# Every transfer on one queue: dt and dt·u stored chunk by chunk, and a schedule drawn anew

## The chip, the core and the metric

The kernel runs on one core of one Trainium2 chip. The core has a matrix engine (PE, with its weight loads PEld), a vector engine (DVE), an activation engine (ACT), a general engine (POOL) and a queue engine (SP) that only issues transfers. They work side by side, each in the order in which its instructions were written, and wait for each other through semaphores. Transfers are issued by SP, ACT or POOL and carried out by 16 DMA engines. The metric is the device time of one execution in microseconds.

## The reference, cut to what matters

The input is x, 4 x 384 x 32 x 32. Two layers follow each other, each with a state-space scan and a feed-forward part, with layer norms and residual sums around them.

```python
# layer 0: four scan directions over 1024 positions, 384 channels, 16 states
x_dbl = einsum('bkdl,kcd->bkcl', xs, x_proj_weight)         # dt rows, B, C
dt = softplus(einsum('bkrl,kdr->bkdl', dts, dt_projs_weight) + bias)
def step(h, inp):
    dtt, ut, bt, ct = inp
    dA = exp(dtt[..., None] * A)
    h = h * dA + (dtt * ut)[..., None] * bt[:, :, None, :]
    return h, einsum('bkdn,bkn->bkd', h, ct)
# ... sum of directions, layer norm, gelu; then t + ffn(ln(t))
# layer 1: in_proj to 2 x 768, causal conv of 4 taps, silu, the same scan over
# 768 channels, * silu(z), out_proj, layer norm; then a mixture of experts:
# softmax gate over 4 experts, the best 2, gelu(x w1 + b1) w2 + b2, weighted sum
```

Everything is in float32.

## The kernel before, in words

**The scan.** The work of both layers' scans is cut into 48 passes. A pass is one batch item, one direction (layer 0) or one group of 384 channels (layer 1), and one half of 512 positions. A pass has three chunks of 128 channels, and a chunk has four steps, each for 4 of the 16 states; that makes 576 steps. In a step the 128 partitions hold 32 channels x 4 states, and four quarters x of the chunk's channels lie side by side. The step consists of

- POOL: `s = dtus * bt` (L1778, called b),
- ACT: `da = exp(dts * a)` for each of the four quarters (L1784, a decay), into one PSUM bank per quarter,
- DVE: one scan per quarter (L1793), then the products with `ct` (L1842); POOL takes one or two of the four products instead (L1858), as the planner decides,
- PE: four sums over the states into `acc` (L1814). After the chunk's last step DVE gathers `acc` (L666 to L672, L918).

**The data of a pass.** `prep_quad0` and `prep_quad1` make, once for two passes, the rows dt, B and C of a direction by a matmul on PE (L637 with the weights `wx0`; L899 in layer 1). ACT copies the result to `xd` (L642), and `rows_out` (L491) stores it to DRAM. `ask_quad0` (L648) loads `wx0` for the next quad as soon as the pass it depends on is prepared; `wx0` has one buffer. `prep_pass` (L520) makes dt (PE L529, softplus in several ACT passes, and a sum on DVE L562 or PE), and dt·u on POOL (L568), each as a tile of 128 x 3 x 512. `spread_out` (L511) stores such a tile in DRAM in the order in which the steps read it, in four transfers of 192 KB, each of 32 partitions and all three chunks. `spread_pass` (L575) loads them back, spread over the states: dt·u of a chunk in one transfer of 1 MB on SP (L590, two buffers), dt of a chunk in two halves of 512 KB on ACT's queue (L596, three buffers). The second half of a chunk goes into the buffer that the first half of the chunk before has used, so it can be asked for only after the second decay of that chunk's last step.

**The order.** Nothing is ordered by hand. `Plan` (L167) draws up the program: it knows a duration for every step, keeps a time for each engine, and emits, one after the other, the instruction that can start first. The scan's own instructions are streams; all else (norms, convolutions, feed-forward, experts, the preparation of passes) are side steps, written as generators that say `yield engine, duration` before they emit. A side step goes in where the planner sees room. `land(kb)` is the planned time of a transfer. `Free` hands out buffers. `fill` adds small matmuls (L1833) to PE's planned gaps. What the planner decides is only the order on each engine; on the chip, semaphores do the waiting. The transfers of SP and ACT take eight completion semaphores in turn, so a transfer is issued only once the eighth before it has landed.

**The experts.** Their blocks (L1386, L1420, L1442) run beside the scan as far as there is room. What is left after the last scan step runs alone at the end, with weights that SP loads (L1355).

Of the kernel before, what the change touches and what calls it, by code (L numbers as in the profile page):

```python
# [133 lines left out]

class Lane:
# [18 lines left out]
    def ready(self):  # L154
        return max(self.want[2] if len(self.want) > 2 else self.end, self.floor) + SLACK[self.rank >= LOW][self.want[0]]
# [11 lines left out]
class Plan:  # L167
# [4 lines left out]
    def __init__(self, streams, jobs, choose, fill):  # L172
# [4 lines left out]
        self.now = 0.0  # L177
        self.stuck = 0.0
# [28 lines left out]
    def mains(self, e):  # L207

        out = []
        for k in range(len(self.streams.get(e, ()))):  # L210
            op = self.head(e, k)
            if op is not None and all(d in self.end for d in op.deps):
                t = max([self.end[d] + LAG for d in op.deps], default=0.0) + op.lag
                out.append((max(self.free[e], t), k, op))
        return out
# [18 lines left out]
    def run(self):  # L234
        while True:
# [22 lines left out]
            start, what, e = best  # L258
            self.stuck = max(self.stuck, start)
# [4 lines left out]
            if isinstance(what, Lane):  # L264
                cost = what.want[1]
# [4 lines left out]
                what.go(what.end, start)  # L270
            else:
# [4 lines left out]
                op.emit()  # L276


@with_exitstack
def layers(ctx, tc, ins, out, const):  # L280
# [160 lines left out]

    def layernorm(src, dst, eps, sq=None, sq_at=0.0, centred=False, scaled=True):
# [41 lines left out]
    def wload(src):  # L484
# [3 lines left out]
        nc.sync.dma_start(out=w.rearrange("p c m -> p (c m)"), in_=src)  # L488
        return w

    def rows_out(q, to):  # L491

        q["rows"] = q.get("rows") or dram.tile([2 * NS, L], F32, tag="rows", name="rows", bufs=4)
        nc.scalar.dma_start(out=q["rows"][:, to], in_=xd[q["at"] : q["at"] + 2 * NS, to])
# [12 lines left out]
    def load_dtw(q, k):  # L507

        nc.sync.dma_start(out=dtw[dt_rows(q), :], in_=ins["w_dt1"][:, k * D : (k + 1) * D])

    def spread_out(to, of):  # L511

        for q in range(NG):
            nc.sync.dma_start(out=to[:, :, q, :].rearrange("c r t -> r c t"), in_=of[q * QP : (q + 1) * QP])
# [5 lines left out]
    def prep_pass(v, p, of_u):  # L520
# [25 lines left out]
        if sums_on_pe(v):  # L546
            yield ACT, 1.5
            nc.scalar.activation(dtu, dtu, AF.Ln, bias=1.0)
            for c in range(NC):
# [6 lines left out]
                ps.give(pd)  # L556
        for c in () if sums_on_pe(v) else range(NC):
# [6 lines left out]
        spread_out(spread[0], dt)  # L564
        for c in range(NC):
            yield POOL, 1.3 if len(of_u(dt[:, c, :], c)) == 1 else 1.75
            for (to, u), (by, _) in zip(of_u(dtu[:, c, :], c), of_u(dt[:, c, :], c)):
                nc.gpsimd.tensor_tensor(to, by, u[:, c], ALU.mult)  # L568
        tmp.give(dt)
        t = yield SP, land(768)  # L570
        spread_out(spread[1], dtu)
# [3 lines left out]
    def spread_pass(p):  # L575
# [3 lines left out]
        def gen():  # L579
            spread, stored = st.pop(("spread", p))  # L580
            for part in range(NC):
# [8 lines left out]
                nc.sync.dma_start(out=dtus[n % 2].rearrange("p q t -> p (q t)"), in_=of(1, 0, NG))  # L590
                plan.end["dtu", p, part] = plan.now + land(1024)
                for x in range(2):
                    m = 2 * n + x - 3
                    before = (yield from until(("da", 4 * (m // 2) + 3, 2 * (m % 2) + 1))) if m >= 0 else 0.0
                    yield ACT, 0.55, max(before, stored)
                    nc.scalar.dma_start(out=dts[(2 * n + x) % 3].rearrange("p q t -> p (q t)"), in_=of(0, 2 * x, 2))  # L596
# [5 lines left out]
    def prep0(b):  # L602
        u = st[("u0", b)]

        def ln(h):
            def gen():
                yield SP, land(768)
                nc.sync.dma_start(out=u[h], in_=half(x_in[b], h))
# [20 lines left out]
    def prep_quad0(q, b, k):  # L629
        def gen():  # L630
# [9 lines left out]
            for h in range(NT):  # L640
                yield ACT, 0.6
                nc.scalar.copy(xd[q["at"] : q["at"] + QROW + R0, cols(h)], px[h * HP : h * HP + QROW + R0])  # L642
            rows_out(q, slice(0, L))
            ps.give(px)
# [3 lines left out]
    def ask_quad0(q, k):  # L648
        def gen():
            yield SP, land(66)  # L650
            nc.sync.dma_start(out=wx0.rearrange("p c m -> p (c m)"), in_=ins["w_x0"][k])
            nc.sync.dma_start(out=dtw[dt_rows(q), :], in_=ins["w_dt0"][k])
# [21 lines left out]
    def post0(b, h):  # L674
# [15 lines left out]
        def add_x(c):  # L690
            def gen():
                xh = yield from t1.take()
                yield SP, land(256)
                nc.sync.dma_start(out=xh, in_=piece(x_in[b], c, h))
# [8 lines left out]
        def ln2():  # L703
# [8 lines left out]
            nc.sync.dma_start(out=fold[:, :, :32], in_=fold_d)  # L712
# [14 lines left out]
        def ffn(lane):  # L727
            def gen():
# [6 lines left out]
                for i in range(2 * lane, 2 * lane + 2):  # L735
                    w, proj1 = yield from wts.two()
                    yield SP, land(192) + 2.0
                    nc.sync.dma_start(
                        out=w.rearrange("p a m -> p (a m)")[zrow, :], in_=ins["w_fc1"][:, i * NC * P : (i + 1) * NC * P]
                    )  # L740
                    nc.sync.dma_start(
# [29 lines left out]
        def ffn_out():  # L771
# [4 lines left out]
            nc.sync.dma_start(out=spread.rearrange("p a m -> p (a m)"), in_=of)  # L776
# [12 lines left out]
            nc.sync.dma_start(out=half(x1[b], h), in_=y)  # L789
# [11 lines left out]
    def prep1(b, h):  # L801
# [6 lines left out]
        def conv(i):  # L808
            def gen():
                for j in range(NC):  # L810
# [8 lines left out]
                    nc.sync.dma_start(out=dg, in_=taps_d[c])  # L819
# [33 lines left out]
        def gate(i):  # L853
            def gen():
# [14 lines left out]
                nc.scalar.dma_start(out=to.rearrange("(c p) t -> p c t", p=P), in_=z)  # L869
# [16 lines left out]
    def prep_quad1(q, b, h):  # L886
        def gen():
# [3 lines left out]
            nc.sync.dma_start(out=wx1, in_=ins["w_x1"].rearrange("p (c m) -> p c m", c=NI))  # L891
# [1215 lines left out]
```

## Time and profile before

| | us |
|---|---|
| three runs | 5034.54, 5049.6, 5051.74 (median 5049.6) |
| the profiled execution | 5032.81 |
| its span, first to last instruction | 5031.0 |
| busy in the span: PE, DVE, POOL, ACT | 4262.9, 4159.0, 4006.4, 3037.3 |
| scan steps (about 110 to 4515 us): DVE busy | 4072.76 of 4405 |
| last experts (4515 to 5031 us): PE busy | 509.12 of 516 |

The transfers move 899.33 MB, 179 GB/s over the span. SP's queue carries 704.28 MB of them (q1) and ACT's 166.22 MB (q10). The page gives for each group of instructions its busy time, the mean of one, and the idle time of the engine just before them with what ended it; a line such as `A <- B: 92.5, 39, 14.1` in the list of waits says that A waited for B 92.5 us in all, in 39 places, at most 14.1 us at once.

### The profile page before, as it was taken

To read this page: it belongs to the slowest core of one execution; us is meant where nothing else is said; L and a number is where in the kernel's file an instruction comes from. 1 tells how busy PE (TensorE), PEld (TensorE's weight loads), DVE (VectorE), ACT (ScalarE), POOL (GpSimd) and SP (SyncE) were. 2 spreads that over 40 slices of the span, in tenths; PEclk is the share of its full clock that TensorE was granted. 3 is DMA by queue.
4 is the path that set the end of the run, shared out by engine and by line. 5 is a ranking of instruction groups with operands and counts; after the bars stand their busy time and mean duration, and the time that the engine had idled before them with its cause. 6 is when DMAs were issued, how large, how long until landed. Compare 5 with 4: busy or idle time off the path is not lost. (4 is left out here: it accounts for less than half of the span.)

```text
span 5031.0 us, 57132 instructions
## 1 busy us (share of the span) xinstructions
PE 4262.9 (85%) x17967; PEld 2192.9 (44%) x17967; DVE 4159.0 (83%) x5754; ACT 3037.3 (60%) x4769; POOL 4006.4 (80%) x1826
## 2 busy tenths in 40 slices
PE   8777778887767799988877798899888888899999
PEld 3222222222223454444444454345534333569996
DVE  4999999999999899999989999999999999850002
ACT  4544458765545577767654577767685756554442
POOL 2999999999988898989988988889899988850002
PEclk9887889888888899999987899899988889899998
DMA  4344656654443565556564655466655454655556
GB/s 148 110 161 156 205 169 214 207 185 139 161 143 107 195 193 175 190 188 211 188 221 161 215 181 175 155 197 205 230 179 191 155 181 148 220 184 180 170 165 190
DMA packets 394191, 899.33 MB, mean 179 GB/s; under 512 B 62384, under 2 KB 143520, under 8 KB 375456
## 3 DMA queue, kind: packets, MB, share of 16 engines
q1 hardware_dynamic: 336672, 704.28, 43.3%
q10 hardware_dynamic: 49024, 166.22, 9.7%
q0 software_dynamic: 8192, 25.17, 1.6%
q8 instruction: 143, 2.34, 0.2%
q14 instruction: 160, 1.31, 0.1%
HBM read 712.11 MB, written 183.40 MB: 178 GB/s over the span
## 5 line engine op out<-in xcount | busy, mean ns | idle before, releaser
L1778 POOL TENSOR_TENSOR s<-dtus,bt 128x2048 f32<-128x2048 f32 x576 | 2605.3, 4533 | 178.1 <-PE acc L1814 67.2
L1784 ACT ACTIVATE da<-dts,a 128x512 f32<-128x512 f32 x2304 | 1530.2, 686 | 886.4 <-DVE s L1842 771.5
L1814 PE MATMUL acc<-s,four 128*32 128x512 f32 x4608 | 735.1, 682 | 382.0 <-POOL s L1858 344.9
L1858 POOL TENSOR_TENSOR s<-s,ct 128x512 f32<-128x512 f32 (+1 forms) x552 | 942.5, 1708 | 138.6 <-DVE s L1793 102.0
L1793 DVE TENSOR_TENSOR_SCAN da<-da,s 128x512 f32<-128x512 f32 x775 | 918.2, 1216 | 114.0 <-ACT da L1784 82.4
L1842 DVE TENSOR_TENSOR s<-da,ct 128x512 f32<-128x512 f32 x1529 | 1009.6, 680 | 0.1
L1793 DVE TENSOR_TENSOR_SCAN da<-da,state,s 128x512 f32<-128x512 f32 x754 | 939.5, 1277 | 17.7 <-ACT da L1784 10.1
L1833 PE MATMUL acc<-ident,few 128*32 128x256 f32 x2886 | 751.5, 416 | 36.2 <-DVE big L918 18.6
L1833 PEld LDWEIGHTS acc<-ident,few 128*32 128x32 f32 x2886 | 334.4, 119 | 510.6 <-issue 225.1
L1793 DVE TENSOR_TENSOR_SCAN s<-da,state,s 128x512 f32<-128x512 f32 x398 | 495.5, 1267 | 8.7 <-ACT da L1784 8.6
L1793 DVE TENSOR_TENSOR_SCAN s<-da,s 128x512 f32<-128x512 f32 x377 | 447.1, 1204 | 17.3 <-ACT da L1784 17.3
L1814 PEld LDWEIGHTS acc<-s,four 128*32 128x32 f32 x4608 | 106.5, 113 | 748.9 <-POOL s L1858 547.3
L1420 PE MATMUL ps<-tmp,mw 128*128 128x256 f32 (+1 forms) x1812 | 387.9, 369 | 22.3 <-ACT tmp L1465 11.5
L1442 PE MATMUL ps<-mw,tmp 128*128 128x192 f32 x2096 | 377.1, 337 | 17.5 <-DMA mw<-in_w_dram 6.8
L1442 PEld LDWEIGHTS ps<-mw,tmp 128*128 128x128 f32 x2096 | 350.4, 195 | 82.4 <-issue 42.9
L1420 PEld LDWEIGHTS ps<-tmp,mw 128*128 128x128 f32 x1812 | 316.5, 198 | 135.7 <-issue 30.4
L1615 DVE SCALAR_TENSOR_TENSOR big<-big,gk,da 128x384 f32<-128x384 f32 x2 | 1.2, 612 | 414.2 <-PE da L1613 414.2
L1605 POOL DMA_INDIRECT big<-ys,slot x12 | 11.8, 980 | 382.7 <-DMA ys<-t 379.3
L799 PE MATMUL ps<-big,w 128*128 128x512 f32 x576 | 280.2, 627 | 14.3 <-DMA w<-in_w_in_dram 8.2
L568 POOL TENSOR_TENSOR tmp<-tmp,big 128x256 f32<-128x256 f32 (+1 forms) x186 | 193.0, 1063 | 68.3 <-DVE tmp L1037 68.3
L529 PE MATMUL ps<-xd,dtw 12*128 12x512 f32 (+1 forms) x288 | 187.9, 743 | 17.2 <-ACT tmp L542 9.4
L838 PE MATMUL ps<-tmp,t 128*128 128x512 f32 x368 | 175.3, 620 | 15.6 <-ACT tmp L830 9.9
(448 smaller groups left out, 5322.2 us busy)
## 6 DMA issues: line engine op xcount, KB each, us to landing
mw<-in_w_dram SPq DMA_DIRECT2D x414, 384.0 KB
dts<-dts ACTq DMA_DIRECT2D x288, 512.0 KB
dtus<-dts SPq DMA_DIRECT2D x144, 1024.0 KB
dts<-tmp SPq DMA_DIRECT2D x376, 192.0 KB
bt<-rows SPq DMA_DIRECT2D x192, 256.0 KB
ct<-rows SPq DMA_DIRECT2D x192, 256.0 KB
dts<-in_w_dram SPq DMA_DIRECT2D x78, 384.0 KB
ys<-t SPq DMA_DIRECT2D x32, 768.0 KB
```

The source lines that it names most:

```text
L529: nc.tensor.matmul(pd, lhsT=dtw[dt_rows(q), c * P : (c + 1) * P], rhs=xd[dt_rows(q), cols(h)], start=True, stop=True,)
L568: nc.gpsimd.tensor_tensor(to, by, u[:, c], ALU.mult)
L799: nc.tensor.matmul(pi, lhsT=w[:, c, :], rhs=u[:, c], start=c == 0, stop=c == NC - 1)
L1420: nc.tensor.matmul(ph[:, k * width : (k + 1) * width], lhsT=w[:, c, k * P : (k + 1) * P], rhs=turned[:, c], start=c == 0, stop=c == NC - 1,)
L1442: nc.tensor.matmul(py[:, k * HD : (k + 1) * HD], lhsT=by_f(hids[half_], width)[:, at_, k * P : (k + 1) * P], rhs=w[:, f], start=4 * q + f ...
L1778: nc.gpsimd.tensor_tensor(ss[i % NSR], dtus[part_of(i) % 2], rep(bts[i % 4], NG), ALU.mult)
L1784: nc.scalar.activation(das[x], dts[(2 * part_of(i) + x // 2) % 3][:, x % 2, :], AF.Exp, scale=v["a"][:, g, m : m + 1])
L1793: nc.vector.tensor_tensor_scan(d if in_psum else s, d, s, 0.0 if v["first"] else state[:, v["slot"], j, x : x + 1], ALU.mult, ALU.add)
L1814: nc.tensor.matmul(acc[x * QP : (x + 1) * QP, :], lhsT=four, rhs=ss[i % NSR][:, x, :], start=m == 0, stop=m == 3)
L1833: nc.tensor.matmul(acc[:QP, : 2 * P], lhsT=nil.to_broadcast([P, QP]), rhs=rep(ident, 2), start=fresh, stop=fresh)
L1842: nc.vector.tensor_tensor(ss[i % NSR][:, x, :], das[x], cts[i % 4], ALU.mult)
L1858: nc.gpsimd.tensor_tensor(s[:, m:, :], s[:, m:, :], rep(cts[i % 4], NG - m), ALU.mult)
```

## The change

All transfers but the indirect ones of POOL are issued by SP: the dt loads, the stores of `rows` and the stores of `z` leave ACT's queue. Each is issued through `ask`, which also tells a model of the queue, `Ring`, about it: SP needs 0.55 us to issue a transfer in the plan, and a transfer can't be issued before the eighth one before it has landed. The planner takes that into account when it asks when SP is free. `spread_out` stores one chunk of 128 channels at a time (256 KB, 128 partitions, with the four quarters as the outer dimension in DRAM), as soon as that chunk is made. In the preparation of a pass the next chunk's step then follows the planned end of the store before it. The planned time of a transfer is slightly shorter, and every side step's duration in the plan is multiplied by a random factor between 0.99 and 1.01 (seed 9; twelve such draws exist).

```diff
+class Ring:
+    at = busy = 0.0
+    lands = [0.0] * 8
+    n = 0
...
+    def next(cls):
+        return cls.lands[cls.n % 8] + 0.1
...
+    def issue(cls, kb):
+        t = max(cls.at, cls.next())
+        cls.busy = max(t + 1.2, cls.busy) + kb / RATE
+        cls.lands[cls.n % 8] = cls.busy + 1.0
+        cls.n += 1
+        cls.at = t + ISSUE
+SEED, SPREAD = 9, 0.02
...
     def ready(self):
-        return max(self.want[2] if len(self.want) > 2 else self.end, self.floor) + SLACK[self.rank >= LOW][self.want[0]]
+        least = Ring.next() - LAG if self.want[0] == SP or len(self.want) > 3 else 0.0
+        return max(self.want[2] if len(self.want) > 2 else self.end, self.floor, least) + SLACK[self.rank >= LOW][self.want[0]]
...
-                cost = what.want[1]
+                cost = what.want[1] * (1.0 + SPREAD * (self.draw.random() - 0.5))
...
+                self.free[e] = max(self.free[e], Ring.at) if Ring.at > start else self.free[e]
...
+    def ask(queue, out, in_):
+        Ring.issue(int(np.prod(out.shape)) / 256)
+        queue.dma_start(out=out, in_=in_)
...
-        nc.scalar.dma_start(out=q["rows"][:, to], in_=xd[q["at"] : q["at"] + 2 * NS, to])
+        ask(nc.sync, out=q["rows"][:, to], in_=xd[q["at"] : q["at"] + 2 * NS, to])
...
-    def spread_out(to, of):
-        for q in range(NG):
-            nc.sync.dma_start(out=to[:, :, q, :].rearrange("c r t -> r c t"), in_=of[q * QP : (q + 1) * QP])
+    def spread_out(to, of, c):
+        ask(nc.sync, out=to[c].rearrange("r q t -> q r t"), in_=of[:, c])
...
                 nc.scalar.copy(dt[:, c, :], pd)
                 ps.give(pd)
+                yield SP, land(256)
+                spread_out(spread[0], dt, c)
...
             nc.vector.tensor_tensor(dt[:, c, :], dt[:, c, :], pd, ALU.add)
             ps.give(pd)
-        spread_out(spread[0], dt)
+            made = plan.free[DVE]
+            yield SP, land(256), made
+            spread_out(spread[0], dt, c)
...
                 nc.gpsimd.tensor_tensor(to, by, u[:, c], ALU.mult)
+            t = yield SP, land(256)
+            spread_out(spread[1], dtu, c)
         tmp.give(dt)
-        t = yield SP, land(768)
-        spread_out(spread[1], dtu)
...
-                    yield ACT, 0.55, max(before, stored)
-                    nc.scalar.dma_start(out=dts[(2 * n + x) % 3].rearrange("p q t -> p (q t)"), in_=of(0, 2 * x, 2))
+                    yield SP, land(512), max(before, stored)
+                    ask(nc.sync, out=dts[(2 * n + x) % 3].rearrange("p q t -> p (q t)"), in_=of(0, 2 * x, 2))
...
-            rows_out(q, slice(0, L))
             ps.give(px)
+            yield SP, land(128)
+            rows_out(q, slice(0, L))
...
-                nc.scalar.dma_start(out=to.rearrange("(c p) t -> p c t", p=P), in_=z)
+                yield SP, land(768)
+                ask(nc.sync, out=to.rearrange("(c p) t -> p c t", p=P), in_=z)
...
 def land(kb):
-    return 3.5 + kb / 200
+    return 3.2 + kb / 220
+RATE, ISSUE = 220.0, 0.55
```

Every other `nc.sync.dma_start` becomes `ask(nc.sync, ...)` with the same operands.

## The prediction

> **What bounds the kernel now.** First the page's busy shares and slices, then the stretches, then the waits.
>
> ```profile
> span 5031.0 us, 57132 instructions
> PE 4262.9 (85%) x17967; PEld 2192.9 (44%) x17967; DVE 4159.0 (83%) x5754; ACT 3037.3 (60%) x4769; POOL 4006.4 (80%) x1826
> ...
> DVE  4999999999999899999989999999999999850002
> ```
> ```profile
> 110.00:4515.00 4405.00, 3663.59 (x14969) 1716.39 (x14970) 4072.76 (x5444) 2772.59 (x4326) 3942.11 (x1763) 0.89 0.55 180
> 4515.00:5031.00 516.00, 509.12 (x2711) 439.78 (x2709) 42.68 (x125) 214.72 (x361) 43.14 (x43) 0.96 0.58 175
> ```
>
> Columns of the second: stretch, length, busy PE, PEld, DVE, ACT, POOL, granted clock, DMA share, GB/s. There are two stages. For 4405 us the 576 scan steps run: DVE is busy 4073 us and sets the pace (7.65 us a step), POOL 3942 us. Then 516 us of expert blocks, in which PE alone is busy (99%). DVE idles 332 us in the first stage. That is what the change can win, and any new wait of DVE is what it can lose. Who makes DVE wait:
>
> ```profile
> ACT xd L642 <- PE ps L637: 106.8, 14, 15.7
> ...
> PE ps L637 <- DMA wx<-in_w_x_dram: 93.8, 12, 14.9
> DVE da L1793 <- ACT da L1784: 92.5, 39, 14.1
> ...
> ACT da L1784 <- DMA dts<-dts: 35.0, 14, 6.5
> ```
>
> (total us, times, longest). The first three are one chain. Its longest case, from the timeline of four engines:
>
> ```profile
> 1664.21 8.83 SPq L514 DMA_DIRECT2D dts<-tmp  x4
> 1673.09 0.43 SPq L651 DMA_DIRECT2D wx<-in_w_x_dram  x1
> ```
> ```profile
> 1675.43 5.41 PE L637 MATMUL ps<-big,wx 128*44 128x256 f32 x24 [12.04 <-DMA wx<-in_w_x_dram]
> ```
> ```profile
> 1680.88 0.58 ACT L642 COPY xd<-ps 44x512 f32<-44x512 f32 x1 [15.65 <-PE ps L637]
> ```
> ```profile
> 1683.57 2.35 DVE L1793 TENSOR_TENSOR_SCAN da<-da,s 128x512 f32<-128x512 f32 x2 [14.12 <-ACT da L1784]
> ```
>
> POOL finishes the three dt·u products at 1662.2; SP needs 8.8 us for four stores, then asks for wx; PE waits for it, ACT waits in order at the xd copy with the next decays behind it, and DVE runs dry. Ten of the layer-0 quads cost DVE 4.8 to 14.1 us in this way, 77 us together (gaps of DVE beside those copies).
>
> **The change part by part.**
>
> (a) ACT no longer issues 328 transfers. Rows: 288 at 0.52 us (L596), 24 at 0.33 (L494), 16 z stores at about 0.4: 165 us of ACT's queue. ACT is busy 63% of the first stage, so this is mostly cover for nothing; DVE waits on ACT for 118 us (92.5 and 25.8), of which 55 belong to the quads. ACT's work in front of DVE becomes 6% less: -8 us (0 to -20).
>
> (b) The quad chain. In the changed order the products of a pass no longer stand in one run on POOL but one per scan step, each followed by its own store, and wx is asked for after one store of 256 KB instead of four of 192 KB. In the trace, wx lands 8.4 us after the last product in the ten bad cases (5.4 to 13.1); with one store (0.4 us of issue) and wx (0.5) I expect about 7. But the order moves PE's quad and ACT's copy as far as it moves POOL: before, the copy stands 0.2 steps behind POOL's last product in the ten bad cases and 1.0 to 9.5 steps behind it in the four good ones; after, it stands -0.5 to +0.5 steps behind in thirteen of fourteen. So the ten win 1.4 us each, and quads 8, 15 and 18, which had room, lose it (3 x about 6 us). +5 us; ends -77 (all ten go) and +50.
>
> (c) The dts loads, 512 KB, now on SP. The first halves have room: 24.5 us (median) from landing to use. The second halves don't: their buffer is free only after the second decay of the chunk's last step. Today ACT issues them 0.03 us (median) later, they land in 5.45 us (90%: 8.23), and DVE would notice if the landing came 5.8 us later (median; 2.9 for the tightest tenth). From these 144 margins, one lateness for all costs DVE 5.5 us at 2 us, 16 at 3, 43 at 4, 87 at 5, 151 at 6. Two things make them late. *Queueing on SP*: SP serves in order, so a load waits for whatever its predecessors wait for, and behind it wait dtus, ct and mw loads. By position in the order, only 6 of the 144 stand behind a producer that is later than the decay that frees their buffer, each by at most half a step; so this is small. *The stores*: their DRAM side now has an outer dimension of 4. The trace has such a transfer: w<-spread_d (192 KB, eight times) is completed by five semaphore increments where others have sixteen, so four channels carry it, and it lands in 5.70 us (median) where w<-in_w_in_dram, of the same size, takes 3.74. A 2048-byte packet takes 0.105 us, so 288 stores put 32 x 0.105 x 288 = 968 us on four channels, where 384 stores put 6 x 0.105 x 384 = 242 us on each of sixteen. Mean share of those four in the first stage: 0.55 + 726/4405 = 0.71. A dts load now waits about 1.8 us (5.45 less the fastest 3.67); as share/(1 - share) this doubles, 2 us more. If the extra is scattered exponentially with mean 2 us, the margins give 144 tight loads 30 us; with mean 1, 5 us; with mean 4, 153. I take +30, ends 0 and +153.
>
> [...]
>
> (d) The chunk stores lengthen the preparation of a pass, for each next chunk waits in the schedule for the last one's store. POOL's last product comes 0 to 4 steps (before: 3 to 7) ahead of the freeing of the buffer for the pass's first dtus load in most passes. A store of 6 us and a load of 7.1 us are two steps, and POOL runs 2.5 steps ahead of DVE, so that covers. Passes 24, 26 and 46, 4 to 5 steps late today, cost 6.8, 2.0 and 12.6 us; after, 24, 26 and 34 are 3 late, 46 is 4, 47 is 2. 0 us (-20 to +30).
>
> (e) Last stage: after the last scan sum PE has 8 more expert matmuls (0.337 us) and 4 transposes: +3 us. The rest there is the same.
>
> (f) Rows and z stores on SP, `ps` given back earlier, 83 fewer filler matmuls, 4% fewer transfers: off the path, 0. They are covered by PE's idle time (4405 - 3664 us) and SP's waits; were that cover gone, 83 x 0.42 = 35 us of PE.
>
> (g) Durations drawn anew by up to 1%: the instructions' counts per engine stay within 0.1% on DVE (1527 products for 1529), so only small stalls move: 0 +- 20.
>
> **Sum.** -8 + 5 + 30 + 0 + 3 = +30 us on the profiled 5032.8 us (span 5031.0), so 5063. The median of the runs shown, 5049.6, is 17 us above that execution; on it, 5080.
>
> **The rivals.** R1, the four channels become the bound: second halves land 4 to 5 us later throughout (+43 to +87), wx 3 us later in 13 quads (+39), so about +95 net: 5145. For it: DMA shares of 0.6 and more in 13 of the 40 slices, where the four would stand above 0.75; each issue also needs the eighth transfer before it to have landed (SP waited 58.7 us for dts loads at the stores). Against: the six stores of a pass are now a step apart. It decides once the second halves land in over 10 us.
> R2, the other side: the schedule now reckons with SP's issue time and its eight transfers in flight, and the quads' stalls go (-77), with (c) as forecast: -8 - 77 + 30 + 3 = -52: 4998. For it: PE's quads stand mostly two to six scan sums later. Against: POOL's products moved as far. It decides if ACT comes to the copy over 12 us after the last product (today 1 to 11).
> R3, spaced stores disturb nothing: -8 + 5 + 3 = 0: 5050.
> That the change doesn't do what it says is excluded by the order: no transfer is left on ACT, 288 stores stand singly.
>
> **How the numbers follow.** My sum 0.40 (its own range 5050 to 5115), R1 0.20, R2 0.20, R3 0.20. About 25 us (0.5%) is what a measurement tells from no change. Faster by more: R2 0.20, R3 0.04, the sum's low end 0.03: 0.27. Within: R3 0.12, the sum 0.14: 0.26. Slower: the rest, 0.47. The range leaves out 0.08 below R2's middle less 10, and 0.1 above R1: 4985 to 5150.
>
> **What would show it.** Right: ACT has no transfers; ACT's wait for dts grows from 35 us to 60 to 120; wx waits of PE stay at 70 to 130 us; stores end with four increments and land in over 5.5 us; the last stage stays 515 to 522 us. Wrong: DVE's gaps at the xd copies gone (R2), or dts waits of several hundred us (R1).

## The result, and the profile after

The changed kernel takes 5054.9 us (median of 21 runs, 5043.2 to 5067.1) where the kernel before takes 5040.4 (median of 21 runs, 5030.6 to 5053.7). The ratio is 1.0026, with a 95% interval of 1.0017 to 1.0035: about 13 us slower. The forecast was 5080 with a range of 4985 to 5150, 30 us above the kernel before. So the sign was right and the size less than half of the forecast; the working behind it was right in less than that, as the experiments show.

The page of the changed kernel, with busy shares and DVE's slices:

```profile
span 5050.0 us, 56868 instructions
PE 4243.3 (84%) x17801; PEld 2178.2 (43%) x17801; DVE 4163.3 (82%) x5756; ACT 3031.5 (60%) x4769; POOL 4013.6 (79%) x1847
...
DVE  3999999999998899999999889999999999950002
...
q1 hardware_dynamic: 380704, 870.48, 52.5%
```

There is no queue of ACT any more, q1 (SP) carries what the two carried. DVE's busy time is nearly the same (4163.3 us for 4159.0), and so is the shape of the slices. The stretches, with the columns as before (stretch, length, busy PE, PEld, DVE, ACT, POOL, clock, DMA share, GB/s):

```profile
110.00:4515.00 4405.00, 3613.55 (x14670) 1682.05 (x14668) 4082.36 (x5452) 2766.31 (x4323) 3951.88 (x1790) 0.89 0.54 179
```

The same 4405 us hold 10 us more of DVE's work mostly because the scan stage now reaches further. Measured by its own marks it is this, in us of the profiled executions:

| | before | after | |
|---|---|---|---|
| first scan starts | 99.4 | 102.5 | +3.1 |
| first scan to last scan | 4373.3 | 4383.1 | +9.8 |
| last scan to the end | 558.3 | 564.4 | +6.1 |
| DVE's gaps over 0.3 us in the scan stage | 276.4 | 280.4 | +4.0 |
| of these beside the xd copies of layer 0 | 77.5 | 67.3 | -10.2 |

The waits, for the whole span:

```profile
DVE da L1840 <- ACT da L1831: 112.9, 45, 29.4
...
ACT xd L686 <- PE ps L681: 105.4, 16, 12.0
...
PE ps L681 <- DMA wx<-in_w_x_dram: 77.8, 13, 9.1
...
ACT da L1831 <- DMA dts<-dts: 46.8, 16, 8.6
```

The chain wx, quad, xd copy, decay, scan is there as before (93.8, 106.8 and 92.5 us then). The 29.4 us of the first line is one wait ahead of the first scan; before, DVE waited there 23.6 us for POOL. ACT's wait for the dts loads rose from 35.0 to 46.8 us and not to the 60 to 120 us that were forecast. One quad of the changed kernel, from the timeline of four engines:

```profile
455.00 0.52 SPq L481 DMA_DIRECT2D dts<-tmp  x1
455.62 0.42 SPq L481 DMA_DIRECT2D wx<-in_w_x_dram  x1
...
461.49 5.40 PE L681 MATMUL ps<-big,wx 128*44 128x256 f32 x24 [8.09 <-DMA wx<-in_w_x_dram]
...
466.93 1.17 ACT L686 COPY xd<-ps 44x512 f32<-44x512 f32 x2 [8.81 <-PE ps L681]
...
468.73 2.34 DVE L1840 TENSOR_TENSOR_SCAN s<-da,s 128x512 f32<-128x512 f32 x2 [4.89 <-ACT da L1831]
```

SP is quick now: one store, and wx is asked for 0.6 us later. But PE starts only 5.9 us after that. From issue to landing, by the trace's completion events, wx takes 6.06 us in the median (2.80 before), and a store 7.11 (3.85 before, for 192 KB). In all 14 quads that come behind a store, wx lands just after that store, 0.2 us later (0.17 to 0.35). The store ends with five increments, one about 1 us after the issue and four from 5.4 us on. Of wx's sixteen, twelve come before those four in each of the 14, and the last four 0.17 to 0.56 us behind them. DVE loses 4.9 us here.

From the time and the totals of the waits alone one would say: nothing much happened, rival R3 came, spaced stores disturb nothing. That reading is wrong.

### The profile page after: what moved, and what is told of

It reads as the page before. It is cut to its first block, busy times and chain, and to the rows that moved or that the text cites. A ratio compares the mean times of both kernels' runs of the same rounds, so it can differ in the third digit from the quotient of the medians.

```text
span 5050.0 us, 56868 instructions
## 1 busy us (share of the span) xinstructions
PE 4243.3 (84%) x17801; PEld 2178.2 (43%) x17801; DVE 4163.3 (82%) x5756; ACT 3031.5 (60%) x4769; POOL 4013.6 (79%) x1847
## 5 line engine op out<-in xcount | busy, mean ns | idle before, releaser
L1861 PE MATMUL acc<-s,four 128*32 128x512 f32 x4608 | 722.4, 671 | 364.3 <-POOL s L1905 348.8
L1880 PE MATMUL acc<-ident,few 128*32 128x256 f32 x2720 | 713.0, 416 | 62.1 <-DVE big L965 26.8
L1880 PEld LDWEIGHTS acc<-ident,few 128*32 128x32 f32 x2720 | 313.1, 119 | 513.9 <-issue 213.5
L1489 PE MATMUL ps<-mw,tmp 128*128 128x192 f32 x2152 | 397.8, 341 | 8.5 <-ACT tmp L1535 5.9
L1489 PEld LDWEIGHTS ps<-mw,tmp 128*128 128x128 f32 x2152 | 367.2, 199 | 85.6 <-issue 42.2
L612 POOL TENSOR_TENSOR tmp<-tmp,big 128x256 f32<-128x256 f32 (+1 forms) x183 | 191.8, 1061 | 75.8 <-DVE tmp L1084 66.9
L844 PEld LDWEIGHTS ps<-big,w 128*128 128x128 f32 x576 | 111.5, 205 | 190.5 <-issue 139.2
```

The lines of the kernel that those rows point to most:

```text
L844: nc.tensor.matmul(pi, lhsT=w[:, c, :], rhs=u[:, c], start=c == 0, stop=c == NC - 1)
L1489: nc.tensor.matmul(py[:, k * HD : (k + 1) * HD], lhsT=by_f(hids[half_], width)[:, at_, k * P : (k + 1) * P], rhs=w[:, f], start=4 * q + f ...
L1861: nc.tensor.matmul(acc[x * QP : (x + 1) * QP, :], lhsT=four, rhs=ss[i % NSR][:, x, :], start=m == 0, stop=m == 3)
L1880: nc.tensor.matmul(acc[:QP, : 2 * P], lhsT=nil.to_broadcast([P, QP]), rhs=rep(ident, 2), start=fresh, stop=fresh)
```

## Experiments

Each series has its own runs of the kernel before, and the ratios are to those. In the series whose kernel before stood near 5065 us, every kernel lost some 24 us in its last 60 us (see the end); 1% is 50 us. Stages and gaps are those of the profiled executions.

**Width of the stores.** `quarter`: the same stores, in the same place of the order, on sixteen channels (each ends with sixteen increments instead of five).

```diff
-        ask(nc.sync, out=to[c].rearrange("r q t -> q r t"), in_=of[:, c])
+        Ring.issue(256)
+        for q in range(NG):
+            nc.sync.dma_start(out=to[c, :, q, :], in_=of[q * QP : (q + 1) * QP, c])
```

> The changed kernel with each 256 KB store issued as four stores of 32 rows by 2 KB (64 KB each), in the same place of every engine's order; nothing else moves. It puts the stores back on sixteen channels and gives SP three more issues a store (288 x 3 at about 0.45 us). Theory N (the four channels are what delays the transfers behind the stores, and that delay is part of the 19 us): the store lands in under 5 us instead of 7.1, wx goes from 6.1 us back to about 3, the first halves of dts from 7.8 to about 6.2, PE's wait for wx falls by 13 x 2 to 3 us, and the time falls by 15 to 40 us against the changed kernel, to some 5015 to 5040 us, that is 0 to 25 us below the kernel before. Theory O (the 19 us come from where the instructions now stand, the narrow stores cost nothing that DVE notices): landings get shorter all the same, but the time stays within 8 us of the changed kernel's 5054.9, or rises by up to 15 us where the longer issue (1.3 us before each wx) is on the path.

Measured: 5014.6 us against 5065.4, ratio 0.9901 (0.9886 to 0.9915), so 63 us below the changed kernel, at the same order on all five engines. The scan stage is 4325.1 us, 58 less. Waits, and the same quad:

```profile
ACT xd L688 <- PE ps L683: 73.7, 16, 9.4
PE ps L683 <- DMA wx<-in_w_x_dram: 40.1, 9, 7.2
...
ACT da L1833 <- DMA dts<-dts: 26.6, 9, 6.6
```

```profile
445.99 1.71 SPq L556 DMA_DIRECT2D dts<-tmp  x4
447.80 0.37 SPq L481 DMA_DIRECT2D wx<-in_w_x_dram  x1
...
450.00 5.41 PE L683 MATMUL ps<-big,wx 128*44 128x256 f32 x24 [5.62 <-DMA wx<-in_w_x_dram]
...
457.24 2.34 DVE L1842 TENSOR_TENSOR_SCAN s<-da,s 128x512 f32<-128x512 f32 x2 [2.39 <-ACT da L1833]
```

wx is asked for 1.2 us later than with one store, and PE starts 2.5 us earlier: 4.0 us from the first store instead of 6.5. wx lands in 2.06 us (median). DVE's gaps at the quads go from 67.3 to 34.6 us, all others from 213.1 to 191.8. Theory N holds, with more than it asked for, and R3 is out: the narrow stores cost the changed kernel 63 us. By landing times (medians, `quarter` to the changed kernel, same order) the width delays wx from 2.06 to 6.06 us, the input weights from 3.27 to 6.33, the convolution's taps from 3.83 to 6.94, the first halves of dts from 6.81 to 7.77 and the second from 4.86 to 5.33.

`narrow_before`: the narrowness alone, in the order of the kernel before.

```diff
-        for q in range(NG):
-            nc.sync.dma_start(out=to[:, :, q, :].rearrange("c r t -> r c t"), in_=of[q * QP : (q + 1) * QP])
+        for c in range(NC):
+            nc.sync.dma_start(out=to[c].rearrange("r q t -> q r t"), in_=of[:, c])
```

> The kernel before with one edit: where a tile of dt or dt u is stored by four transfers of 192 KB on sixteen channels, three of 256 KB with an outer dimension of 4 stand in the same place. Every engine's order stays, the dts loads stay on ACT. It is the narrowness by itself. Theory N: three stores back to back put 96 rows of 2 KB on each of four channels, about 10 us, so that the last of a tile's stores lands after 9 to 12 us in place of 4 to 6; wx behind them lands 3 to 6 us later at the quads (+30 to +60 us), first halves of dts and dtus of a new pass likewise, second halves up to 2 us: in all +30 to +80 us, a ratio of 1.006 to 1.016. Theory that narrow stores cost only in the new order or with the loads on the same queue: 0.998 to 1.003.

Measured: 5295.9 against 5065.0, ratio 1.0444 (1.0430 to 1.0459), about 225 us slower, nearly three times the top of what was expected. Waits:

```profile
ACT xd L642 <- PE ps L637: 188.3, 16, 24.8
PE ps L637 <- DMA wx<-in_w_x_dram: 177.3, 12, 21.2
```

The three stores, back to back, land in 10.57 us (median), wx behind them in 10.82. Gaps at the quads double (77.5 to 157.1 us) and all others grow from 198.8 to 350.4. So the changed kernel gets off cheaply, with stores that stand a step apart.

**The queue.** `dts_sp`: the kernel before, its 288 dts loads on SP.

```diff
-                    nc.scalar.dma_start(out=dts[(2 * n + x) % 3].rearrange("p q t -> p (q t)"), in_=of(0, 2 * x, 2))
+                    nc.sync.dma_start(out=dts[(2 * n + x) % 3].rearrange("p q t -> p (q t)"), in_=of(0, 2 * x, 2))
```

> The kernel before with one edit: the 288 dts loads are issued on SP, at the place in the order that they had on ACT. Stores still in fours on sixteen channels, z and rows still on ACT. It is terms (a) and (c) of the prediction without the narrow stores. Theory Q (a single in-order queue makes second halves late): their landing after the freeing of the buffer grows from 5.5 us by 1 to 3 us, ACT's wait for dts grows from 35 to over 60 us, and the time rises by 5 to 30 us over 5040. Theory F (the queue itself is free, ACT is relieved): second halves within 0.5 us of before, ACT's 150 us of issuing gone, time 0 to 15 us below 5040. A third possibility: loads that wait on SP hold back wx behind them at the quads, which would show as a longer wait of PE for wx (over 110 us against 94).

Measured: 5036.0 against 5065.4, ratio 0.9946 (0.9934 to 0.9959): 27 us faster, beyond the 0 to 15 of theory F. First scan 8.6 us earlier, scan stage 14.9 shorter, of which 9.6 at the quads. The cause is not separated further: ACT no longer issues 288 loads, and the second halves also land sooner.

```profile
ACT xd L642 <- PE ps L637: 97.7, 14, 14.0
DVE da L1793 <- ACT da L1784: 80.6, 35, 12.0
PE ps L637 <- DMA wx<-in_w_x_dram: 75.9, 11, 10.4
...
ACT da L1784 <- DMA dts<-dts: 31.2, 12, 9.1
```

Nothing became late: the second halves are issued up to 0.7 us after their buffer is free in three quarters of cases (0.03 before) and land 4.80 us after the issue in the median (5.45 before). The first halves land later, 7.08 us for 6.18, but they have room; over all loads the median is the same (5.86 for 5.87). Queueing costs nothing that DVE feels here.

`whole`: the changed kernel with the stores of before (four of 192 KB, once a pass); the order is planned anew.

```diff
-    def spread_out(to, of, c):
-        ask(nc.sync, out=to[c].rearrange("r q t -> q r t"), in_=of[:, c])
+    def spread_out(to, of):
+        for q in range(NG):
+            ask(nc.sync, out=to[:, :, q, :].rearrange("c r t -> r c t"), in_=of[q * QP : (q + 1) * QP])
...
-            yield SP, land(256), made
-            spread_out(spread[0], dt, c)
+        yield SP, land(768), made
+        spread_out(spread[0], dt)
...
-            t = yield SP, land(256)
-            spread_out(spread[1], dtu, c)
+        t = yield SP, land(768)
+        spread_out(spread[1], dtu)
```

> The changed kernel with the stores of before: each of dt and dt u once a pass, as four stores of 192 KB on sixteen channels, when all three chunks are done; the queue's model in the schedule, SP alone and the drawn durations stay. The order is planned anew. Theory N (narrow stores cost about 60 us, SP alone gains about 25): ratio 0.990 to 0.997, near the 0.9946 of the kernel before with its dts loads on SP. If storing the chunks singly is itself a gain (the 0.990 of the four small stores a chunk against 0.9946), this one is 0.994 to 0.998. Theory O (the new order is what costs): 1.000 to 1.005.

Measured: 4939.7 against 5040.6, ratio 0.9798 (0.9780 to 0.9817): 101 us below the kernel before, twice what the boldest theory had (0.990). DVE's gaps at the quads are 16.7 us.

`whole_noring`: `whole` without the model of the queue.

```diff
     def ask(queue, out, in_):
-        Ring.issue(int(np.prod(out.shape)) / 256)
         queue.dma_start(out=out, in_=in_)
```

> The changed kernel with four stores a pass and seed 9 (ratio 0.980), and without the model of SP's queue in the schedule: issuing takes no time there and nothing waits for the eighth transfer before, as in the kernel before. SP alone and the drawn durations stay. Theory P (the schedule's knowledge of the queue is a gain of its own): ratio 0.990 to 1.000, back at the 0.9946 that SP alone gave to the kernel before. Theory S (the gain comes with SP's single queue or with the drawn order): 0.975 to 0.986.

Measured: 4996.1 against 5039.4, ratio 0.9911 (0.9893 to 0.9930), 57 us above `whole`; at the lower edge of theory P. The waits in the scan stage, first `whole`, then without the model:

```profile
ACT xd L685 <- PE ps L680: 44.8, 10, 6.8
...
PE ps L680 <- DMA wx<-in_w_x_dram: 27.1, 9, 6.3
```

```profile
ACT xd L684 <- PE ps L679: 105.4, 12, 20.2
...
PE ps L679 <- DMA wx<-in_w_x_dram: 87.7, 12, 13.1
```

Gaps at the quads: 16.7 with the model, 71.1 without. The schedule that knows SP's queue does take the quads' stalls away, as rival R2 said, here with one seed. Most of that time comes back elsewhere: all other gaps of DVE in the scan stage grow from 163.4 to 209.7 us, of which one wait is

```profile
DVE s L1888 <- DMA ct<-rows: 22.3, 1, 22.3
```

The scan stage is 25 us shorter with the model. Another 32 us of the 57 stand in the last stretch, from the last scan to the end (533.2 us for 565.1): some 84 fewer expert matmuls are left for it.

`before_draw9`: drawn durations alone in the kernel before.

```diff
-                cost = what.want[1]
+                cost = what.want[1] * (1.0 + 0.02 * (self.draw.random() - 0.5))
```

> The kernel before with durations of the side steps drawn within 1% (seed 9), nothing else: loads of dts on ACT, four stores a pass. If the drawn order is a gain by itself: 0.975 to 0.990. If a draw is worth no more than between the seeds tried so far (1.0026, 1.0087 and 1.0063 in the changed kernel, 0.980 and 0.976 with four stores a pass): 0.996 to 1.006.

Measured: 5019.3 against 5039.4, ratio 0.9962 (0.9948 to 0.9976), 19 us faster.

**The draw.** `draw1` and `draw2` are the changed kernel with other seeds, `whole_draw1` is `whole` with seed 1, and `after_again` is the changed kernel once more.

```diff
-SEED, SPREAD = 9, 0.02
+SEED, SPREAD = 1, 0.02      # draw2: 2
```

> The changed kernel with another seed for the durations of the side steps (1 in place of 9); everything else as changed. This is term (g), 0 +- 20 us in the prediction. If the draw is a small matter: a ratio to the kernel before of 0.998 to 1.007. If the draw alone moves the time by as much as the four stores a pass did (a ratio of 0.980 in place of 1.002), it could be anywhere from 0.975 to 1.025, and then the order, not the stores, would be the reading of that run.

> The changed kernel with seed 2. As for the run with seed 1: 0.998 to 1.007 if the draw is small; the distance between the seeds 9, 1 and 2 is the measure of what one draw is worth.

> The changed kernel with the stores of before (four of 192 KB, once a pass, on sixteen channels), and seed 1. With seed 9 it stood at a ratio of 0.980. Theory N (the narrow chunk stores cost the changed kernel its gain): 0.975 to 0.987 again, and at least 60 us below the changed kernel with the same seed. Theory of the lucky draw: 0.99 to 1.005, near the changed kernel with the same seed. The stretch after the last scan was 533 us with seed 9 and 564 in the changed kernel, with some 146 fewer matmuls left in it; if that is luck, it will be 550 to 570 here.

> The changed kernel itself, beside the next three. In the first call the kernel before stood at 5065.4 us where it had stood at 5040.4, and the last stage of all four kernels was some 24 us longer than in the first traces; the ratios alone can be compared between calls. If nothing but the chip differs, the ratio to the kernel before is again 1.001 to 1.004 and the scan stage again some 10 us longer than before.

Measured: `draw1` 5109.5 against 5065.0, ratio 1.0087 (1.0071 to 1.0102); `draw2` 5097.1, 1.0063 (1.0048 to 1.0078); `whole_draw1` 4942.6, 0.9757 (0.9742 to 0.9771); `after_again` 5052.6 against 5040.6, 1.0020 (1.0009 to 1.0031). The changed kernel with seed 1 is 31 us above itself with seed 9, with seed 2 it is 19 above: a draw is worth some 20 to 30 us. Much of that is single waits: DVE waits 29.5 us at a sum of an expert's output and 18.4 us for POOL in `draw1`, 31.9 us for POOL in `draw2`, and nowhere more than 9.3 us in the scan stage with seed 9. All three seeds are slower than the kernel before. The stores once a pass are worth 115 us with seed 9 and 166 with seed 1. That is no draw's luck; the short last stretch of `whole` (533 us) was, for with seed 1 it is 581 in a series that adds 24.

**Single chunks.** `chunks_only`: the kernel before with nothing but narrow stores of single chunks, planned anew.

```diff
+    def spread_out(to, of, c):
+        nc.sync.dma_start(out=to[c].rearrange("r q t -> q r t"), in_=of[:, c])
...
-        spread_out(spread[0], dt)
+            yield SP, land(256), made
+            spread_out(spread[0], dt, c)
...
-        t = yield SP, land(768)
-        spread_out(spread[1], dtu)
+            t = yield SP, land(256)
+            spread_out(spread[1], dtu, c)
```

> The kernel before with only the chunks of dt and dt u stored singly, in one narrow store of 256 KB each; dts loads, rows and z stay on ACT, durations as they were, no model of the queue. The order is planned anew. Theory N: the narrow stores cost here what they cost in the changed kernel, without SP's gain: ratio 1.005 to 1.012. Rival (on ACT's own queue the dts loads escape the stores, and it was the shared SP queue that made them costly): ratio 0.997 to 1.003, with first halves of dts landing in about 6 us as before and not in 7.8.

Measured: 5097.9 against 5040.6, ratio 1.0109 (1.0093 to 1.0126). First scan 12.7 us later, scan stage 77 longer (34.4 of it one wait of DVE for POOL), last stretch 21 shorter. The dts loads, on ACT's own queue, land in 6.75 us (all, median) where they took 5.87: a queue of their own does not save them from the stores.

`quarter_draw1` is `quarter` with seed 1. `quarter_free` and `quarter_free_draw1` take the waits between the chunks of a pass out of the schedule:

```diff
-            yield SP, land(256), made
+            yield SP, 0.5, made
...
-            t = yield SP, land(256)
+            t = yield SP, land(256) if c == NC - 1 else 0.5
```

> The changed kernel with each chunk store as four of 64 KB on sixteen channels, and seed 1. With seed 9 the width of the stores was worth 63 us (0.990 against 1.0026), and from there to four stores a pass another 52 (0.980). If both are effects of the edits and not of one order: here 0.993 to 0.999 (1.0087 less 0.0125, give or take 0.003), some 90 us above four stores a pass with seed 1 (0.976), so that the finer stores themselves cost 50 to 110 us. If the second step was the draw's, this kernel falls to 0.975 to 0.985.

> The chunk stores on sixteen channels (ratio 0.990 with seed 9), and in the schedule a pass no longer waits for the landing of one chunk's store before it prepares the next: each store is booked with 0.5 us for the pass, only the last one with its landing of 4.4 us. It tests term (d), the longer preparation, which the prediction put at 0. If the waits between chunks are why single chunks cost 52 us over four stores a pass (0.980): 0.978 to 0.984. If not (more transfers on SP, or where the expert blocks came to stand): 0.987 to 0.995.

> The same with seed 1, where single chunks on sixteen channels gave 0.994 and four stores a pass 0.976. If the waits between chunks are the cause: 0.974 to 0.982. If not: 0.989 to 0.998. If the two seeds disagree, the draw hides it and the cause stays open.

Measured: `quarter_draw1` 5012.3 against 5039.4, ratio 0.9941 (0.9920 to 0.9961); `quarter_free` 5019.5 against 5063.9, 0.9906 (0.9888 to 0.9924); `quarter_free_draw1` 5010.3, 0.9883 (0.9862 to 0.9903). So at full width the single chunks still cost 52 and 93 us over `whole`. Without the waits it is 54 and 63: nothing gained with one seed, 29 us with the other. The waits are at most a part of it. By stages of the profiled executions (24 us taken off the last stretch in the series that add them) the cost is:

| | to the first scan | scan stage | last stretch |
|---|---|---|---|
| `quarter` less `whole` (seed 9) | +11 | +17 | +31 |
| `quarter_draw1` less `whole_draw1` (seed 1) | +9 | +77 | +8 |

So more than half of the 52 is the short last stretch of `whole` again. DVE's gaps in the scan stage are the same in `quarter` and `whole` (226.5 and 226.4 us); with seed 1, one wait of 27.0 us at a sum of an expert's output is in the 77. Whether the rest is the number of transfers on SP (24 for a pass instead of 8) or the place of other work stays open.

**The quads.** `early_after`, `early_before`, `early_quarter` and `early_whole` (on `whole_draw1`) ask for wx and dtw early and keep the order of all else. `load_wx` and `load_dtw0` are the two transfers that stood in `ask_quad0`; there, only the first quads' are left.

```diff
+    def next_dtw(q, p):
+        n = q["n"] + 2
+        if p == q["p"] + 1 and n < len(quads) and not quads[n]["layer"]:
+            load_dtw0(quads[n])
...
             spread_out(spread[0], dt, c)
+            if c == 0:
+                next_dtw(q, p)
...
             rows_out(q, slice(0, L))
+            later0 = [r for r in quads if not r["layer"] and r["n"] > q["n"]]
+            if later0:
+                load_wx(later0[0])
```

> The changed kernel with the loads of wx and dtw for a layer-0 quad moved ahead: wx is asked for behind the rows store of the quad before, dtw behind the first store of the pass that reads its rows last. All other instructions keep their order. Theory W (the chain last product, store, wx, quad, xd copy, decay makes DVE idle at 13 quads): PE's wait for wx (78 us) vanishes, ACT's wait at the xd copy (105 us) falls below 30, DVE's gaps at the quads (some 60 us together) fall below 20, and the time falls by 40 to 60 us, to about 5000. Rival (the quad would wait for something else that comes as late, its ps buffer or the slot of xd): the wait at the xd copy stays above 70 us and the time falls by less than 15 us.

> The same early loads of wx and dtw in the kernel before (wx behind the rows store of the quad before, dtw behind the store of dt). If the quads' stalls are what was read from its trace (ten quads, 77 us of DVE's time) the time falls by 55 to 77 us, to some 4965 to 4985, and so by about 15 us more than in the changed kernel, where they cost DVE some 60. If the rival holds (something else as late), less than 15 us. If both early kernels end within 10 us of each other, the 15 us between the two kernels lie in the quads; if they keep the 15 us between them, the quads have no part in the result.

> The changed kernel with both edits: four stores of 64 KB on sixteen channels for each chunk, and wx and dtw asked for early. Alone they gave ratios of 0.990 and 0.993 to the kernel before, against 1.0026 of the changed kernel, so 63 and 49 us. The first already brought wx 4 us sooner and took 32 us off ACT's wait at the xd copy, so the two overlap: theory N with W expects 75 to 95 us below the changed kernel, a ratio of 0.983 to 0.988. If the whole of the narrow stores' cost lay in the quads, the two would give no more than the larger of them: 0.990. If they add in full: 0.980.

> The best so far (four stores a pass, seed 1, ratio 0.9757) with wx and dtw for the quads asked for early; all other instructions in the same order. ACT waits 60 us at the xd copies there, of which DVE feels less than half: 10 to 35 us faster, a ratio of 0.969 to 0.974. If ACT's lead over DVE covers those waits: 0.974 to 0.977.

| | time, before | ratio (95%) | quads' gaps | all other gaps |
|---|---|---|---|---|
| changed kernel | 5054.9, 5040.4 | 1.0026 (1.0017 to 1.0035) | 67.3 | 213.1 |
| `early_after` | 5027.9, 5065.4 | 0.9928 (0.9916 to 0.9941) | 3.5 | 234.4 |
| `early_before` | 4999.1, 5065.4 | 0.9870 (0.9856 to 0.9884) | 5.4 | 215.1 |
| `early_quarter` | 4979.7, 5040.6 | 0.9884 (0.9863 to 0.9904) | 3.3 | 189.8 |
| `early_whole` | 4905.3, 5039.4 | 0.9729 (0.9713 to 0.9745) | 2.8 | 164.1 |

The quads' stalls go in all four. `early_before` gains 66 us of the 77.5 that stood there, `early_after` 49 of 67.3; some 16 to 21 us come back as other gaps. The two end 29 us apart, though their quads are now alike; their other gaps differ by 19 us. So the quads are not what sets the changed kernel above the one before. `early_quarter` is some 70 us below the changed kernel (72 by the ratio in the table, 68 by that of `after_again` in the same series), less than the 75 to 95 expected; the two edits overlap in wx. With wx asked for early, the width of the stores is worth 22 us (0.9928 to 0.9884) instead of 63, which is what wx as the main victim asks for; the gaps in the table say 45, but the profiled execution of `early_quarter` is the fastest of six, 16 us below their median. `early_whole` gains 14 us by the ratios, 22 by the gaps, and is the fastest version found, some 135 us below the kernel before.

## Why the prediction was wrong, and what of it was right

In ratios, and 50.4 us for each 1%, the way from the kernel before to the changed one is:

| step, by the two runs that differ in it | us |
|---|---|
| dts loads on SP (`dts_sp`) | -27 |
| rows and z on SP, planned landing times, seed 9 (`whole_noring` less `dts_sp`) | -18 |
| the queue's model in the schedule (`whole` less `whole_noring`) | -57 |
| single chunks, at full width (`quarter` less `whole`) | +52 |
| the stores' four channels (changed kernel less `quarter`) | +63 |
| sum | +13 |

The first, and the last, are at an unchanged order; the three between were planned anew, and each carries a draw's 20 to 30 us. The model's -57 and the single chunks' +52 share the short last stretch of `whole`, 32 and 31 us of them; without it they are some -25 and +21, and the sum hardly changes. Five steps of 18 to 63 us come to 13. The forecast saw three of them (ACT's issues, the narrow stores and, as a rival, the queue's model), and its sum came near by luck as much as by working.

- **(a) ACT relieved, -8.** The direction was right and the size was not: -27 with everything else in place, though sooner second halves may have a part in it. 8.6 us of it lie ahead of the first scan, where the prediction counted nothing.
- **(b) The quads, +5.** Measured: -10. The prediction expected wx about 7 us after the last product; in the changed kernel it is 6.4 to 7.4 us in most quads, as forecast. What it did not see is that 4 of the 6 us from wx's issue to its landing are the narrow store in front of wx. At full width wx lands 3.7 to 4.0 us after the product in most quads, with four times the issues.
- **(c) Late second halves, +30.** This is the step that failed. The stores were rightly read as four-channel transfers from w<-spread_d, they end with five increments as that did, and four of wx's sixteen come late behind them. But the forecast made the second halves 2 us later, scattered over all 144 loads. They land in 5.33 us, no later than before (5.45) and 0.5 us later than at full width (4.86), and late ones cost DVE some 5 us in either kernel. In the changed kernel 23 of the 144 second halves are issued right behind a store; these land in 7.07 us (median), the others in 5.25. Disturbed are, by `quarter`, above all wx (4.0 us later), the input weights (3.1) and the taps (3.1). Most of these have room; wx has none, and from `quarter` to the changed kernel 33 of the 54 us of added gaps stand at the quads. R1 had a term for just that, "wx 3 us later in 13 quads (+39)", and the sum left it out. The right cause, the wrong victim, and half the size: 63 for 30. Two readings under this term were off as well, without weight: the fastest second half lands in 3.44 us, not 3.67, and 0.105 us is the mean time of a 2048-byte packet in the trace of the kernel before, where the median is 0.084.
- The queueing on SP, put at a small cost in (c), was no cost that shows (`dts_sp`).
- **Width and queue, as measured.** The stores with an outer dimension of 4 end with five increments, those of `quarter` with sixteen. What the narrow ones cost is the 63 and 225 us of `quarter` and `narrow_before`. The other issuing engine alone left the landing times as they were (`dts_sp`: 5.86 us over all dts loads, 5.87 before); the kernel is 27 us faster even so, which fits ACT's time in front of DVE (288 issues of 0.52 us before) but was not shown to be that alone.
- **R2, the quads' stalls go, -77.** Its mechanism is real: the model takes them from 71.1 to 16.7 us in `whole`. Its size is not: other gaps grew by 46 us, and the scan stage is 25 us shorter. It was dismissed because POOL's products move as far as the quads; the narrow stores then hid it, so that the changed kernel shows 67.3.
- **(d) 0.** Not supported: single chunks at full width cost 52 and 93 us, 28 and 86 of it up to the last scan. That the preparation's waits do it is not shown either.
- **(e) +3** measured +6.1 between the profiled executions. **(f)** was not tried by itself beyond the rows and z in the table. **(g) 0 ± 20** was a little narrow: 1.0026, 1.0087 and 1.0063 for three seeds, a spread of 31 us, and -19 us in the kernel before.

The forecast of the profile: no transfers on ACT, right; PE's wait for wx between 70 and 130 us, right (77.8); stores of over 5.5 us, right (7.11, with five increments, one more than the outer dimension; the loads of dtw, with twelve rows, end with thirteen); the last stage 515 to 522 us, wrong as read (535 from the same mark, 4515): the scan ends 13 us later, and the stage's own length rose by 6.1; ACT's wait for dts 60 to 120 us, wrong (46.8). The 13 slices that R1 counts with a DMA share of 0.6 or more are 12 on the page.

## What to carry to other kernels

Before pricing a transfer, look at how many increments complete it: here a store whose outer dimension is 4 (five increments, where the same stores of `quarter` have sixteen) held back what was issued right behind it on SP's queue (wx 6.06 us for 2.06), and in `chunks_only` the loads on ACT's landed later too (6.75 us for 5.87). The one to price is the transfer behind it that has no room, not the largest or the tightest set. A bundle of changes that measures as nothing can hold 100 us in each direction; undo the parts one at a time at an unchanged order before believing that none of them matters. Where an engine waits in order for something that needs a weight, load that weight a stage early: here that was worth 66 us in the kernel before and 49 in the changed one, but only 9 on `quarter` and 14 on `whole_draw1`, where wide stores, and in the second the schedule, had removed much of the stall already.

## What the runs showed of the hardware that was not expected

- A transfer of 66 KB that ends with sixteen increments (wx) takes 6.06 us behind one store of 256 KB that ends with five, and 2.06 us behind four stores of 64 KB that end with sixteen each, though these need three more issues. Three of the 256 KB stores back to back make it 10.82 us. Behind the one store, wx lands 0.2 us after it in all 14 quads.
- With all loads on one queue instead of two, the dts loads land no later on the whole: second halves in 4.80 us instead of 5.45, first halves in 7.08 instead of 6.18, all in 5.86 instead of 5.87, with the same stores around them (`dts_sp`).
- In three of the five series the kernel before stood some 24 us higher. In the traces of all ten kernels of those series DVE stands idle for 20 to 28 us, in three or four waits, at sums for the output within the last 60 us; in the ten others no wait there is over 2 us once these sums have begun. The last stores to the output, which carry these sums, are spread out with it: SP issues the first four over 25 us in `quarter` and over 7 in the changed kernel, each issue taking 0.4. From the timelines of `quarter` and then of the changed kernel:

```profile
4947.46 25.08 SPq L481 DMA_DIRECT2D out_dram<-big  x4
...
4958.98 0.55 DVE L1674 TENSOR_TENSOR big<-big,ps 128x384 f32<-128x384 f32 x1 [6.98 <-issue]
...
4971.58 0.56 DVE L1674 TENSOR_TENSOR big<-big,da 128x384 f32<-128x384 f32 x1 [12.04 <-issue]
```

```profile
5007.31 6.97 SPq L481 DMA_DIRECT2D out_dram<-big  x4
```

The profile shows nothing that ends these waits, and nothing in the program tells why. No kernel was traced in both kinds of series. Ratios within a series are hardly touched by it, times across series are.
